# Attention scores as one product over 64 rows instead of two passes over 32, with new turn orders

## The chip, the core and the metric

The kernel runs on one core of a Trainium2 chip. The core's engines work side by side: TensorE (PE in the profile, its weight loads PEld) multiplies, VectorE (DVE) and ScalarE (ACT) work on tiles of 128 partitions, GpSimd (POOL) does elementwise work on SBUF, and SyncE (SP) issues most of the transfers. Products land in PSUM, which has eight banks of 128 x 512 fp32; operands lie in SBUF. The metric is the device time of one execution in microseconds. The run before has three times: 1256.90, 1262.49 and 1262.93, median 1262.49.

## The reference

The input is x of 2 x 1024 x 512 fp32. Three layers follow each other:

```
x = x + 0.5 * ffn(layernorm(x))      # base matmul + bias, and a top-2 mix of 8 rank-16 adapters
x = x + attn(layernorm(x))           # 32 heads of width 16, 8 kv heads, so 4 heads share a k and a v
x = x + 0.5 * ffn(layernorm(x))      # the same ffn again
```

The attention's weights are binarized: each is replaced by its sign, and the row's mean absolute value goes into a scale on the output. Scores are `q.k / sqrt(16)` over all 1024 keys, softmax runs over the keys, and the output projection is binarized too. Outputs that are not finite are replaced.

## The kernel before, in words

**Precision.** fp32 products on TensorE take several passes, the `float32r` format one, with fewer bits. So q and k are split: `y` is the value rounded to float32r (high), `o` the rest (low), and the scores are the sum of the four products of the two halves. For a head of width 16, q's high and low halves lie in 32 rows (16 + 16). A k tile `k` has two planes: plane 0 holds the high half of k, plane 1 the low half, each repeated over all rows. A product of 32 rows of q with the low plane and one with the high plane, both added into the same PSUM bank, give all four terms.

**Staging.** The halves of q and k are written to DRAM by `qkv_part` (`qd`: 2D rows, `kd`: P rows and 2S columns) and read back in the layout of the attention by `place` and, for the first unit alone, `place_k`.

**Units and turns.** The attention is cut into 32 units: a batch (2), a block of 512 queries (2) and a kv head (8) with its four heads. A unit has 32 `m` tiles (128 queries x 512 keys of one head, whose maximum over the keys is taken), 32 `e` tiles (128 keys x 512 queries), and 8 x 2 parts `A` of the product with v. The order within a unit is: `m_tile` on TensorE and `m_max` on VectorE (L751) give a maximum per query; `m_gather` and `m_place` turn it, split into two float32r halves, into two rows per head (`mq`); `e_tile` then computes the transposed scores into a bank, adds the negated maximum by a product of two rows of ones with `mq` (L785), and ScalarE takes the exponential from the bank to SBUF (`es`, L787); `a_part` multiplies with v and a column of ones (L820) into one bank `av`, which `unit_end` copies out (`avs`) and stores.

A unit takes TU = 4 turns of its own, and `e` runs LEAD = 5 turns behind `m`, the `A` parts one turn behind `e`, so each turn holds 8 `m` tiles, 8 `e` tiles and 4 `A` parts of up to three units. Seven PSUM banks rotate among `m`, `e` and the background work; `av` has the eighth.

**Orders written out by hand.** Within a turn, the order of instructions is a string. `m0(5)` is pass 0 of the turn's `m` tile 5, `m1(5)` pass 1; `e0`, `e1` are the two passes of an `e` tile and `e2` its product with `mq`; `A0` to `A3` are the parts with v; `S` is `m_place`. Head h = i % 4 of tile i lies in rows 32h to 32h+31, so tiles of four different heads use four different row strips of TensorE. The other letters offer a place to background work: `F` to one of TensorE, `V`/`W` to VectorE, `C`/`D` to ScalarE.

There are three strings: `FULL` where a background strand wants TensorE, `BARE` where none does, `LEAD_IN` for turns that have `m` only. In the program before, 97 turns are full, 32 bare and 3 lead-in.

**Background.** The rest (the ffn, layernorm, projections, normalization and output projection of other token groups) is written as generators ("strands"). A small planner, `Flow`, decides by costs of its own and by stocks of buffers (`stock`, where `t` counts 512-wide scratch tiles) which strand gets the next place. Planning happens while the program is built; on the chip each engine runs its list in order. All transfers of the attention go through SP's queue, in the order in which the planner issues them: in a turn where a unit ends its `m` tiles, `m_place` first, then other strands' stores, and `place` for the next unit at the turn's end. Of POOL's work the attention needs only `vaug`.

**Buffers.** `q`, `k` and `mq` have three buffers each, `es` fourteen, `av` one bank.

Of the kernel before, what the change touches and what calls it, by code (L numbers as in the profile page):

```python
# [8 lines left out]
F32 = mybir.dt.float32  # L9
F32R = mybir.dt.float32r  # L10
# [5 lines left out]
P = 128  # L16
D = 512
KC = D // P
# [5 lines left out]
REP = H // G  # L24
HD = 16
TG = 4
GT = TG * P
# [5 lines left out]
def macaron_kernel(ctx: ExitStack, tc: tile.TileContext, x_in, wbT, b_base, wrT, aT, bT,  # L33
                   wqT, q_sc, wkT, k_sc, wvT, v_sc, woT, o_sc, out):
    nc = tc.nc
    B, S, _ = x_in.shape
# [4 lines left out]
    const = ctx.enter_context(tc.tile_pool(name="const", bufs=1))  # L41
    xpool = ctx.enter_context(tc.tile_pool(name="xres", bufs=B * NG))
    p2 = ctx.enter_context(tc.tile_pool(name="p2", bufs=2))
    tmp = ctx.enter_context(tc.tile_pool(name="tmp", bufs=11))
    sm = ctx.enter_context(tc.tile_pool(name="sm", bufs=4))
    dram = ctx.enter_context(tc.tile_pool(name="dram", bufs=2, space=bass.MemoryType.DRAM))
    ps = ctx.enter_context(tc.tile_pool(name="ps", bufs=7, space=bass.MemoryType.PSUM))
# [5 lines left out]
    def bank(name):  # L53
        return ps.tile([P, 512], F32, tag="w", name=name)
# [75 lines left out]
    class Flow:  # L130
        def __init__(self):
            self.t, self.free, self.strands, self.n = 0, True, [], 0
            self.stock = dict(m=3, n=4, t=10, xT=2, xL=2, hT=1, fb=6)
            self.lock = None
            self.busy = dict.fromkeys("Pvagd", 0)

# [353 lines left out]
    def qkv_part(b, g, xs, i, fast, at):  # L490
# [40 lines left out]
        if i <= KC:  # L531
            yield "a", "v"
            hi = y[:, :].bitcast(F32R)
            nc.scalar.copy(hi, o)  # L534
            yield "v" if fast else "g", "a"
            lo = o[:, :].bitcast(F32R)
            (nc.vector if fast else nc.gpsimd).tensor_tensor(lo, o, y, ALU.subtract)  # L537
            for j, t in enumerate((y, o)):
                dst = (qd[b][i * 2 * P:(i + 1) * 2 * P, cols].rearrange(
                           "(h i d) s -> h i d s", i=2, d=HD)[:, j, :, :] if i < KC  # L540
                       else kd[b][:, j * S + g * GT:j * S + (g + 1) * GT])
                yield ("d", "v" if fast else "g") if j == 0 else ("d", "d")
                nc.sync.dma_start(dst, t)
        flow.give(t=2 if i <= KC else 1)
        ended.add((b, g, i))

# [72 lines left out]
    def o_proj(b, g, hs, rank, mv, given, fast=False):  # L619
# [32 lines left out]
        for t in range(TG):  # L652
# [7 lines left out]

    FULL = ("e0(3) e0(2) m0(5) m0(0) e1(3) e1(2) m1(5) V m1(0) e2(3) e2(2) C e0(1) A0 A1 A2 A3 S "
            "m0(1) m0(6) e0(7) e0(4) m1(1) m1(6) e1(7) W e1(4) e1(1) m0(2) e2(7) e2(4) e2(1) C "
            "m1(2) V F e0(6) e0(0) m0(7) e0(5) e1(6) e1(0) m1(7) e1(5) e2(6) e2(0) D m0(3) e2(5) "
            "m0(4) m1(3) F m1(4)")
    BARE = ("C m0(1) m0(2) e0(3) e0(4) V m1(1) e0(6) e1(3) e1(4) m0(5) e1(6) e2(4) e2(3) m1(5) "
            "m1(2) A0 S e2(6) e0(1) m0(0) e0(7) e1(1) C m1(0) e1(7) W m0(6) e2(1) e0(0) e2(7) m1(6) "
            "A1 e1(0) V m0(7) e0(5) e0(2) e2(0) D m1(7) e1(2) e1(5) m0(4) m0(3) e2(2) e2(5) m1(4) "
            "m1(3) A2 A3")  # L670
    LEAD_IN = ("m0(0) m0(5) m0(2) V m1(0) m1(5) F C V m0(7) m1(2) m1(7) V F C m0(4) m0(1) m0(6) V m1(4) "
               "m1(1) F C V m0(3) V m1(6) S m1(3) F C V")
    FULL, BARE, LEAD_IN = (
        [(o[0], int(o[1]) if len(o) > 1 else 0, int(o[3]) if len(o) > 2 else 0)
         for o in t.split()] for t in (FULL, BARE, LEAD_IN))
    TU = NT // 2
    LEAD = TU + 1
    units = [(b, qb, g) for b in range(B) for qb in range(NQB) for g in range(G)]
# [3 lines left out]
    def place(u):  # L682


        b, qb, g = units[u]
        q = p2.tile([P, 512], F32R, tag="q", name=f"q{u}", bufs=3)
        nc.sync.dma_start(q.bitcast(F32), qd[b][g * P:(g + 1) * P, qb * 512:(qb + 1) * 512])
        k = p2.tile([P, 2, S], F32R, tag="k", name=f"k{u}", bufs=3)
        st[u].update(q=q, k=k, es={}, mq=p2.tile([P, 512], F32R, tag="mq", name=f"mq{u}", bufs=3),
                     mn=p2.tile([P, REP, 4, 2], F32, tag="mn", name=f"mn{u}"))  # L690
        if u:
            nc.sync.dma_start(k.bitcast(F32).rearrange("p i s -> p (i s)"),
                              kd[b][g * HD:(g + 1) * HD, :].unsqueeze(0).to_broadcast(
                                  [P // HD, HD, 2 * S]))

    def place_k(half):

        for i in range(2):
            nc.sync.dma_start(st[0]["k"].bitcast(F32)[:, i, half * 512:(half + 1) * 512],
                              kd[0][0:HD, i * S + half * 512:i * S + (half + 1) * 512]  # L700
                              .unsqueeze(0).to_broadcast([P // HD, HD, 512]))

    def begin():

        yield "u", lambda: {(0, 0, KC), (0, 0, 0)} <= ended
        yield "d", "x"
        place(0)
        place_k(0)
        for j in range(4):
            yield "P", "d" if j == 0 else "", None, 4  # L710
            for p in range(2):
                for h in range(REP):
                    m_tile(0, j * REP + h, p, False)
            for h in range(REP):
                yield "v", "P"
                m_max(0, j * REP + h)
                flow.give(fb=1)
        yield "u", lambda: (0, 1, KC) in ended
        yield "d", "x"
        place_k(1)  # L720

    def place_v(u):

# [8 lines left out]
        step = i // REP  # L732
        return (step % 4, step // 4) if u == 0 else (step // 2, step % 2)

    def m_tile(u, i, p, end=True):

        s = st[u]
        h, (qt, kh) = i % REP, m_where(u, i)
        rows = slice(32 * h, 32 * h + 32)
        if p == 0:  # L740
            s["m", i] = bank(f"m{u}_{i}")
        nc.tensor.matmul(s["m", i], s["q"][rows, qt * P:(qt + 1) * P],  # L742
                         s["k"][rows, 1 - p, kh * 512:(kh + 1) * 512],
                         start=(p == 0), stop=(p == 1))
        if p == 1 and end:
            m_max(u, i)

    def m_max(u, i):
# [23 lines left out]
    def e_tile(u, i, p):  # L772

        s = st[u]
        kt, h = i // REP, i % REP
        rows = slice(32 * h, 32 * h + 32)
        if p == 0:
            s["e", i] = bank(f"e{u}_{i}")
        t = s["e", i]
        if p < 2:  # L780
            nc.tensor.matmul(t, s["k"][rows, 1 - p, kt * P:(kt + 1) * P], s["q"][rows, :],  # L781
                             start=(p == 0), stop=False)
        else:
            two = slice(32 * h, 32 * h + 2)
            nc.tensor.matmul(t, ones_r[two, :], s["mq"][two, :], start=False, stop=True)  # L785
            e = p2.tile([P, 512], F32, tag="es", name=f"es{u}_{i}", bufs=14)
            nc.scalar.activation(e, s.pop(("e", i)), AF.Exp, scale=HD ** -0.5)  # L787
            s["es"][i] = e
# [42 lines left out]
    def attention(chains, n0):  # L831
# [5 lines left out]
        live = []  # L837

        def need(*keys):
            for _ in range(4000):  # L840
                flow.settle()
                if set(keys) <= ended:
                    return
                flow.t += 1
                for kind in "Pvagd":
                    flow.busy[kind] = 0
                    flow.offer(kind)
            raise RuntimeError([(s.rank, s.kind, s.arg) for s in flow.strands])

        for n in range(n0, TU * len(units) + LEAD + 1):  # L850
# [5 lines left out]
            if e and e[1] == 0:  # L856
                need(*[(units[e[0]][0], h, KC + 1) for h in range(NG)])
                place_v(e[0])
            order = (LEAD_IN if not e and not a else FULL if flow.wants("P", begin + TICK * 5 // 8)
                     else BARE)  # L860

            hold = n % TU == 0 and n // TU
            for pos, (kind, p, i) in enumerate(order):
                flow.t = max(flow.t, begin + pos * TICK // len(order))
                if kind == "m":
                    if m:
                        m_tile(m[0], m[1] * 2 * REP + i, p)
                elif kind == "e":
                    if e:
                        e_tile(e[0], e[1] * 2 * REP + i, p)  # L870
                elif kind == "A":
                    if a:
                        a_part(a[0], a[1] * 2 + p // 2, p % 2)
                elif kind == "S":
                    if 0 < hold <= len(units):
                        m_place(hold - 1)
                    hold = 0
                elif kind == "F":
                    flow.offer("P")
                elif kind in "VW":  # L880
                    if kind == "V" or not m or flow.crowd("v") > 1:
                        flow.offer("v")
                elif kind in "CD":
                    if kind == "C" or not e or flow.crowd("a") > 1:
                        flow.offer("a")
                flow.offer("g")
                if not hold:
                    flow.offer("d")
# [9 lines left out]


    qd = [dram.tile([2 * D, S], F32, tag="qd", name=f"qd{b}") for b in range(B)]  # L900
    kd = [dram.tile([P, 2 * S], F32, tag="kd", name=f"kd{b}") for b in range(B)]
    ad = [dram.tile([G * P, S], F32, tag="ad", name=f"ad{b}") for b in range(B)]
    rv = dram.tile([2, P, 512], F32, tag="rv", name="rv", bufs=1)
    rd = [dram.tile([NQB, H, 512], F32, tag="rd", name=f"rd{b}") for b in range(B)]
# [118 lines left out]
```

## Time and profile before

| what | value |
|---|---|
| times of three runs | 1256.90, 1262.49, 1262.93 us |
| profiled execution | 1256.92 us, span 1255.2 us |
| granted TensorE clock, mean over the span | 0.915 |
| PE busy, DVE busy, ACT busy, POOL busy | 1148.8, 902.8, 641.6, 295.0 us |
| first `e` product to last `av` product | 148.9 to 1185.8 us |
| the same stretch: DVE busy, ACT busy, DMA share, granted clock | 759.1 us, 601.3 us, 0.24, 0.93 |
| DMA moved | 85.57 MB |

The span runs from the first to the last instruction; the time of an execution is about 2 us more. A group line gives the engine, operation, tiles (out<-in), count, then busy time and mean length, then the idle time of the engine before such instructions and what ended it. TensorE's products are pipelined and their ends are modelled, so the distance between starts says more than the length. In the chain of waits, each step is followed back to what released it; "issue" is time in which an engine waited for nothing that the profile shows.

### The profile page before, as it was taken

To read this page: it belongs to the slowest core of one execution; us is meant where nothing else is said; L and a number is where in the kernel's file an instruction comes from. 1 tells how busy PE (TensorE), PEld (TensorE's weight loads), DVE (VectorE), ACT (ScalarE), POOL (GpSimd) and SP (SyncE) were. 2 spreads that over 40 slices of the span, in tenths; PEclk is the share of its full clock that TensorE was granted. 3 is DMA by queue.
4 is the path that set the end of the run, shared out by engine and by line. 5 is a ranking of instruction groups with operands and counts; after the bars stand their busy time and mean duration, and the time that the engine had idled before them with its cause. 6 is when DMAs were issued, how large, how long until landed. Compare 5 with 4: busy or idle time off the path is not lost.

```text
span 1255.2 us, 25499 instructions
## 1 busy us (share of the span) xinstructions
PE 1148.8 (92%) x10501; PEld 606.1 (48%) x10501; DVE 902.8 (72%) x1733; ACT 641.6 (51%) x1249; POOL 295.0 (24%) x302
## 2 busy tenths in 40 slices
PE   3988699999999999999999999999999999998868
PEld 3546355454454544444554445444455444545434
DVE  5578876767786777776677976777769677895273
ACT  2222255655554665565565666455557655566401
POOL 3135832000000340031555220241000300422110
PEclk8989588899986999987999899899989899999788
DMA  7010332121212222223132241122222422211110
GB/s 254 1 59 34 81 122 85 52 52 52 52 52 52 69 80 57 70 76 89 49 90 75 72 122 53 33 52 69 61 60 67 123 68 65 68 55 38 45 39 34
DMA packets 38708, 85.57 MB, mean 68 GB/s; under 512 B 7728, under 2 KB 10800, under 8 KB 34624
## 3 DMA queue, kind: packets, MB, share of 16 engines
q1 hardware_dynamic: 37184, 81.26, 22.4%
q8 instruction: 82, 1.34, 0.4%
q10 hardware_dynamic: 1152, 2.10, 0.4%
q0 software_dynamic: 256, 0.59, 0.3%
q14 instruction: 34, 0.28, 0.1%
HBM read 59.57 MB, written 23.84 MB: 66 GB/s over the span
## 4 chain that ended last, share of the span: by engine, by line
PE 70%; DVE 19%; issue 3%; DMA 2%; POOL 2%; ACT 1%; SPq 1%; POOLq 0%; ACTq 0%; DVEq 0%
PE av L820 20%; PE m L742 16%; DVE mn L751 11%; PE e L781 10%; PE pbf L419 5%; PE pbs L419 5%; PE e L785 4%; PE po L634 2%; PE phs L342 1%; DMA qd<-y 1%; PE pq L504 1%; PE pbf L423 1%; PE pv L521 1%; PE pbs L423 1%; DMA x<-in_x 1%
## 5 line engine op out<-in xcount | busy, mean ns | idle before, releaser
L751 DVE TENSOR_REDUCE mn<-m 128x1 f32<-128x512 f32 x1024 | 657.0, 682 | 230.0 <-PE m L742 221.4
L787 ACT ACTIVATE es<-e 128x512 f32<-128x512 f32 x1024 | 546.9, 599 | 425.6 <-PE e L785 401.4
L742 PE MATMUL m<-k,q 32*128 32x512 f32 x2048 | 492.1, 464 | 21.1 <-DVE mn L751 15.1
L781 PE MATMUL e<-q,k 32*128 32x512 f32 x2048 | 407.9, 474 | 8.3 <-DVE mn L751 6.9
L742 PEld LDWEIGHTS m<-k,q 32*128 32x128 f32 x2048 | 240.8, 196 | 153.0 <-issue 67.4
L820 PE MATMUL av<-es,vaug 128*32 128x256 f32 x4096 | 290.3, 416 | 16.4 <-issue 10.3
L781 PEld LDWEIGHTS e<-q,k 32*128 32x128 f32 x2048 | 185.1, 194 | 114.7 <-DVE mn L751 69.6
L785 PE MATMUL e<-mq,ones_r 2*128 2x512 f32 x1024 | 233.0, 431 | 3.7 <-DMA mq<-mT 3.7
L820 PEld LDWEIGHTS av<-es,vaug 128*32 128x32 f32 x4096 | 121.5, 116 | 154.5 <-issue 103.8
L785 PEld LDWEIGHTS e<-mq,ones_r 2*128 2x128 f32 x1024 | 125.6, 196 | 25.1 <-issue 13.7
L419 PE MATMUL pbf<-wb,xTf 128*128 128x512 f32 x128 | 68.9, 653 | 1.3 <-DVE mn L751 1.3
L419 PE MATMUL pbs<-wb,xTs 128*128 128x512 f32 x128 | 64.8, 618 | 1.2 <-DVE mn L751 1.2
L586 POOL TENSOR_TENSOR an<-an,rb 128x512 f32<-128x512 f32 x15 | 19.2, 1281 | 142.7 <-DMA rd<-rs 72.1
L249 POOL TENSOR_SCALAR loa<-y 128x512 f32<-128x512 f32 x17 | 12.7, 750 | 157.1 <-ACT y L509 147.5
L726 POOL MEMSET vaug<- 128x128 f32 x32 | 6.6, 206 | 137.7 <-PE av L820 137.6
L419 PEld LDWEIGHTS pbf<-wb,xTf 128*128 128x128 f32 x128 | 23.2, 203 | 30.1 <-issue 26.1
L419 PEld LDWEIGHTS pbs<-wb,xTs 128*128 128x128 f32 x128 | 21.5, 189 | 27.1 <-issue 22.9
L253 POOL TENSOR_SCALAR z<-y 128x512 f32<-128x512 f32 x17 | 34.1, 2008 | 1.8 <-DMA qd<-y 0.6
L249 POOL TENSOR_SCALAR loo<-yo 128x512 f32<-128x512 f32 x12 | 7.4, 613 | 113.7 <-DVE yo L639 110.0
L537 POOL TENSOR_TENSOR z<-z,y 128x512 fp32r<-128x512 f32 x17 | 21.9, 1293 | 51.0 <-ACT y L534 51.0
L590 POOL TENSOR_TENSOR anxL<-an,anxT 128x512 fp32r<-128x512 f32 x15 | 19.2, 1280 | 53.5 <-ACT anxT L588 53.4
L634 PE MATMUL po<-sign_o,anxT 128*128 128x512 f32 x64 | 29.4, 459 | 1.2 <-DVE mn L751 1.2
(193 smaller groups left out, 1008.3 us busy)
## 6 DMA issues: line engine op xcount, KB each, us to landing
k<-kd SPq DMA_DIRECT2D x31, 1024.0 KB
q<-qd SPq DMA_DIRECT2D x32, 256.0 KB
ad<-avs SPq DMA_DIRECT2D x32, 256.0 KB
x<-in_x SPq DMA_DIRECT2D x16, 256.0 KB
qd<-y SPq DMA_DIRECT2D x16, 256.0 KB
qd<-z SPq DMA_DIRECT2D x16, 256.0 KB
an<-ad SPq DMA_DIRECT2D x15, 256.0 KB
rb<-rd SPq DMA_DIRECT2D x15, 256.0 KB
```

The source lines that it names most:

```text
L249: nc.gpsimd.tensor_scalar(lo_, y, 0.0, -BIG, ALU.min, ALU.max)
L253: nc.gpsimd.tensor_scalar(o, y, 0.0, BIG, ALU.max, ALU.min)
L419: nc.tensor.matmul(pb, xT[:, c, t * P:(t + 1) * P], wb[:, c, :], start=(c == 0), stop=False)
L423: nc.tensor.matmul(pb, hT[0][:, t * P:(t + 1) * P], lb, start=False, stop=True)
L537: (nc.vector if fast else nc.gpsimd).tensor_tensor(lo, o, y, ALU.subtract)
L634: nc.tensor.matmul(po, hs[j][:, c, t * P:(t + 1) * P], wo[:, c, :], start=(c + j == 0), stop=(c + j == KC))
L742: nc.tensor.matmul(s["m", i], s["q"][rows, qt * P:(qt + 1) * P], s["k"][rows, 1 - p, kh * 512:(kh + 1) * 512], start=(p == 0), stop=(p == 1))
L751: nc.vector.tensor_reduce(s["mn"][:, h, qt, kh:kh + 1], s.pop(("m", i)), AX.X, ALU.max, negate=True)
L781: nc.tensor.matmul(t, s["k"][rows, 1 - p, kt * P:(kt + 1) * P], s["q"][rows, :], start=(p == 0), stop=False)
L785: nc.tensor.matmul(t, ones_r[two, :], s["mq"][two, :], start=False, stop=True)
L787: nc.scalar.activation(e, s.pop(("e", i)), AF.Exp, scale=HD ** -0.5)
L820: nc.tensor.matmul(s["av"][32 * h:32 * h + 32, cols], s["v"][:, kt, :], s["es"][kt * REP + h][:, cols], start=(kt + half == 0), stop=(kt + ...
```

## The change

- q's halves lie twice in 64 rows: the tile `q` has a plane for each parity of the head, and heads 0 and 1 use rows 0 to 63, heads 2 and 3 rows 64 to 127. For a head the rows are high, low, high, low of q.
- k lies in 64 rows as high, high, low, low, twice over the partitions, in one plane. One product over 64 rows gives the four terms; the second pass is gone for `m` and for `e`.
- The product with `mq` keeps its two rows in the 32-row strip of the head. It is now `e1`.
- q and k share one buffer of the size that k had. q is loaded by four transfers, each of which reads 32 rows twice; k by one of half the size. `kd` now has 4P rows of S columns, and each half is stored twice, by two transfers.
- The scratch pool has 13 tiles instead of 11, and the planner's stock `t` is 12 instead of 10.
- All three strings are new. In them, `F` stands twice side by side in `FULL`, and `A0` of `BARE` stands near the start of the turn, so the planner first waits until the bank `av` of the unit before has been copied. In the program after, 95 turns are full, 34 bare and 3 lead-in. `FULL` is chosen by the place of its first `F`.

```diff
-    tmp = ctx.enter_context(tc.tile_pool(name="tmp", bufs=11))
+    tmp = ctx.enter_context(tc.tile_pool(name="tmp", bufs=13))
...
-            self.stock = dict(m=3, n=4, t=10, xT=2, xL=2, hT=1, fb=6)
+            self.stock = dict(m=3, n=4, t=12, xT=2, xL=2, hT=1, fb=6)
...
-                dst = (qd[b][i * 2 * P:(i + 1) * 2 * P, cols].rearrange(
-                           "(h i d) s -> h i d s", i=2, d=HD)[:, j, :, :] if i < KC
-                       else kd[b][:, j * S + g * GT:j * S + (g + 1) * GT])
-                yield ("d", "v" if fast else "g") if j == 0 else ("d", "d")
-                nc.sync.dma_start(dst, t)
+                n_ = 2 if i < KC else 4
+                dst = (qd[b][i * 2 * P:(i + 1) * 2 * P, cols] if i < KC else kd[b][:, cols]).rearrange(
+                    "(h i d) s -> h i d s", i=n_, d=HD)
+                for c in range(n_ // 2):
+                    yield ("d", "v" if fast else "g") if j + c == 0 else ("d", "d")
+                    nc.sync.dma_start(dst[:, j * n_ // 2 + c, :, :], t)
...
-    FULL = ("e0(3) e0(2) m0(5) m0(0) e1(3) e1(2) m1(5) V m1(0) e2(3) e2(2) C e0(1) A0 A1 A2 A3 S "
-            "m0(1) m0(6) e0(7) e0(4) m1(1) m1(6) e1(7) W e1(4) e1(1) m0(2) e2(7) e2(4) e2(1) C "
-            "m1(2) V F e0(6) e0(0) m0(7) e0(5) e1(6) e1(0) m1(7) e1(5) e2(6) e2(0) D m0(3) e2(5) "
-            "m0(4) m1(3) F m1(4)")
-    BARE = ("C m0(1) m0(2) e0(3) e0(4) V m1(1) e0(6) e1(3) e1(4) m0(5) e1(6) e2(4) e2(3) m1(5) "
-            "m1(2) A0 S e2(6) e0(1) m0(0) e0(7) e1(1) C m1(0) e1(7) W m0(6) e2(1) e0(0) e2(7) m1(6) "
-            "A1 e1(0) V m0(7) e0(5) e0(2) e2(0) D m1(7) e1(2) e1(5) m0(4) m0(3) e2(2) e2(5) m1(4) "
-            "m1(3) A2 A3")
+    FULL = ("m0(5) V m0(3) C F F e0(4) m0(7) V W e0(1) e0(3) e1(1) e1(4) e0(2) e1(2) e1(3) m0(1) C "
+            "A0 A1 S e0(6) e0(0) e1(6) e0(5) m0(6) e1(0) e1(5) m0(2) D A2 A3 m0(4) e0(7) m0(0) "
+            "e1(7)")
+    BARE = ("e0(0) W m0(2) A0 S C e0(3) e1(0) e0(2) m0(4) e1(2) e1(3) m0(1) A1 A2 m0(0) C m0(7) "
+            "e0(1) e0(6) e0(4) e1(6) e1(4) D e1(1) m0(6) A3 m0(5) V e0(7) e0(5) m0(3) e1(5) e1(7) V")
+    LEAD_IN = ("m0(0) m0(5) m0(2) V m0(7) F C V m0(4) m0(1) V F C m0(6) V F C V m0(3) V S F C V")
...
-        q = p2.tile([P, 512], F32R, tag="q", name=f"q{u}", bufs=3)
-        nc.sync.dma_start(q.bitcast(F32), qd[b][g * P:(g + 1) * P, qb * 512:(qb + 1) * 512])
-        k = p2.tile([P, 2, S], F32R, tag="k", name=f"k{u}", bufs=3)
+        qk = p2.tile([P, 2, S], F32R, tag="k", name=f"k{u}", bufs=3)
+        q, k = qk[:, 0, :].rearrange("p (t s) -> p t s", t=2), qk[:, 1, :]
...
+        for t in range(2):
+            for h in range(2):
+                row = g * P + (2 * h + t) * 32
+                nc.sync.dma_start(q.bitcast(F32)[64 * h:64 * h + 64, t, :],
+                                  qd[b][row:row + 32, qb * 512:(qb + 1) * 512].unsqueeze(0)
+                                  .to_broadcast([2, 32, 512]))
...
+    def place_k(u, s0, s1):
+        b, _, g = units[u]
+        nc.sync.dma_start(st[u]["k"].bitcast(F32)[:, s0:s1],
+                          kd[b][g * 64:(g + 1) * 64, s0:s1].unsqueeze(0).to_broadcast(
+                              [2, 64, s1 - s0]))
...
+    def rows_of(h):
+        return slice(64 * (h // 2), 64 * (h // 2) + 64)
+
+    def m_tile(u, i, end=True):
...
-        nc.tensor.matmul(s["m", i], s["q"][rows, qt * P:(qt + 1) * P],
-                         s["k"][rows, 1 - p, kh * 512:(kh + 1) * 512],
-                         start=(p == 0), stop=(p == 1))
+        nc.tensor.matmul(s["m", i], s["q"][rows_of(h), h % 2, qt * P:(qt + 1) * P],
+                         s["k"][rows_of(h), kh * 512:(kh + 1) * 512], start=True, stop=True)
...
-        if p < 2:
-            nc.tensor.matmul(t, s["k"][rows, 1 - p, kt * P:(kt + 1) * P], s["q"][rows, :],
-                             start=(p == 0), stop=False)
+            nc.tensor.matmul(t, s["k"][rows_of(h), kt * P:(kt + 1) * P], s["q"][rows_of(h), h % 2, :],
+                             start=True, stop=False)
...
                     if a:
+                        if a[0] and a[1] == p == 0:
+                            until(lambda: "av" not in st[a[0] - 1])
                         a_part(a[0], a[1] * 2 + p // 2, p % 2)
...
-    kd = [dram.tile([P, 2 * S], F32, tag="kd", name=f"kd{b}") for b in range(B)]
+    kd = [dram.tile([4 * P, S], F32, tag="kd", name=f"kd{b}") for b in range(B)]
```

## The prediction

> **What bounds the kernel now.** The page's busy lines and its chain come first.
>
> ```profile
> PE 1148.8 (92%) x10501; PEld 606.1 (48%) x10501; DVE 902.8 (72%) x1733; ACT 641.6 (51%) x1249; POOL 295.0 (24%) x302
> ...
> PE 70%; DVE 19%; issue 3%; DMA 2%; POOL 2%; ACT 1%; SPq 1%; POOLq 0%; ACTq 0%; DVEq 0%
> PE av L820 20%; PE m L742 16%; DVE mn L751 11%; PE e L781 10%; PE pbf L419 5%; PE pbs L419 5%; PE e L785 4%; PE po L634 2%; PE phs L342 1%; DMA qd<-y 1%; PE pq L504 1%; PE pbf L423 1%; PE pv L521 1%; PE pbs L423 1%; DMA x<-in_x 1%
> ```
>
> TensorE carries 70% of the chain, the row maximum `mn` (L751) on VectorE 11%, or 0.109 x 1255.2 = 137 us by the finer share of the chain view. The first product of `e` starts at 148.9 us and the last `av` ends at 1185.8 us: 1037 us for 132 turns, 7.86 us each. Next, the chain in order of time inside one full turn (start, us, what):
>
> ```profile
> 293.27 1.87 PE av L820 x32
> 295.14 0.43 PE m L742 x2
> 295.57 0.01 PE e L781
> 295.57 0.23 PE m L742
> 295.80 0.00 PE e L781
> 295.80 0.00 PE m L742
> 295.81 0.22 PE e L781
> 296.03 0.24 PE e L785 x3
> 296.26 0.00 PE m L742
> 296.27 1.06 PE pbf L419 x2
> 297.32 0.42 PE e L781 x2
> ```
>
> Score products come in sets of up to four, one per 32 rows, that start together; sets follow each other at 0.23 us. The first step after `av` or `pbf` costs 0.43 us. So a **change of tile shape** (32x128 score tiles, 128x32 `av`, 128x128 background) costs 0.43 - 0.23 = 0.20 us. The timeline of TensorE shows it product by product (start, length, group):
>
> ```profile
> 602.75 0.50 PE L504 MATMUL pq<-xTa,sign_k 128*128 128x512 f32 x1
> 603.09 0.40 PE L504 MATMUL pq<-xLa,sign_k 128*128 128x512 f32 x1
> 603.32 0.39 PE L504 MATMUL pq<-xTa,sign_k 128*128 128x512 f32 x1
> 603.55 0.40 PE L504 MATMUL pq<-xLa,sign_k 128*128 128x512 f32 x1
> 603.88 0.49 PE L781 MATMUL e<-q,k 32*128 32x512 f32 x2
> 603.88 0.49 PE L742 MATMUL m<-k,q 32*128 32x512 f32 x1
> ```
>
> Inside one shape the starts are 0.23 apart; from `pq` (128 rows) to `e` (32 rows) 0.33, and the step behind a change is 0.34 (602.75 to 603.09): 0.10 + 0.11 = 0.21 us. No change of shape in this trace is free. Two-row `mq` products (L785) beside 32-row ones at 604.45 cost nothing: both fill one 32-row strip. The group lines give what is exchanged:
>
> ```profile
> L742 PE MATMUL m<-k,q 32*128 32x512 f32 x2048 | 492.1, 464 | 21.1 <-DVE mn L751 15.1
> L781 PE MATMUL e<-q,k 32*128 32x512 f32 x2048 | 407.9, 474 | 8.3 <-DVE mn L751 6.9
> L785 PE MATMUL e<-mq,ones_r 2*128 2x512 f32 x1024 | 233.0, 431 | 3.7 <-DMA mq<-mT 3.7
> ```
>
> **The change part by part.**
>
> *Fewer, taller products.* 2048 + 2048 products of a quarter set become 1024 + 1024 of half a set; the 1024 `mq` products keep their quarter. Before: 5120/4 = 1280 full sets; after: 2048/2 + 1024/4 = 1280. Counting through the two built orders, with a new set whenever rows collide or another kind of work comes between, gives 1399 and 1396: 3 x 0.23 = -1 us. 2048 weight loads of 0.19 us go too; they lie beside running products (0.23 us between sets with four loads inside it), so they give 0; were that cover gone, a load would show as the 0.10 us after a change of shape.
>
> *Shape changes already known.* In the two orders the changes among score, `av`, background and `mp` go from 776 to 795 (two background offers now stand side by side, `av` is cut into more pieces): 19 x 0.20 = +4 us.
>
> *Shape changes that are new.* `m` and the first `e` product are now 64 rows high, the `mq` product still lies in 32. The built order goes between the two heights 1199 times (5 groups of `mq` in a full turn, 4 in a bare one, two changes each; 95 full and 34 bare turns). The trace has no such pair. Lower bound 0, from the two-row products above that join 32-row ones for nothing; upper bound 0.20 us each, as every change of shape that it has, plus the sets torn: a 32-row pair can't share a set with a 64-row product then, and the count is 1865 sets for 1396. I take the upper end, since the nearest rows are changes of tile height (128 to 32) and these cost 0.20 without exception: 1199 x 0.20 = 240, 469 x 0.23 = 108, together +348 us.
>
> The Trainium skill, page "TensorEngine Tiling (Array Packing)", section "Tiling Modes", says that a change of tiling mode, not of tile alone, drains TensorE, and lists 64 and 32 rows as different modes. The page "TensorE: Matmul & The Clock Gate", Part 3, says that weight loads pass running products where the row groups differ; by that one alone mixed heights on disjoint rows would cost nothing and the sum would end near the value before.
>
> *Banks.* A score bank of `m` is held for one step less, 0.23 of about 1.5 us (two steps, 0.39 of a product, 0.68 of the reduction), 15%. TensorE's weight loads waited 49.4 + 69.6 us on `mn` and 12.2 + 10.9 us on `es`, 142 us in all: 0 to -142, and 15% of it, -20 us, is what I take where TensorE's own work stays equal. Where it grows by 348/132 = 2.6 us a turn, VectorE's 759/132 = 5.75 us per turn are hidden in 10.5 and most of the 137 us of `mn` on the chain go: bounds 0 and -137, I take two thirds, -91, and nothing for the banks beside it.
>
> *av early in a bare turn.* A0 of a unit now stands near the start of a bare turn and must wait for the copy of the bank before it (`avs`, 0.60 us, behind up to three `es` of 0.60). About 8 of the 32 units start so: 0 to 8 x 2.4 = 19, I take +5 us. Behind the wait stand all later products.
>
> *Loads and stores.* Per unit q comes as four 128 KB loads instead of one of 256 KB, k as 512 KB for 1024; k stores double. Bytes: -31 x 0.5 + 32 x 0.25 + 1 = about -6.5 MB of 85, with the DMA engines at 0.24 in the attention. SP issues three more loads, 0.33 us each (one `q` issue is 0.33, one `k` 0.62): 1 us later for k and for what queues behind, against three turns (23 us) until `m` of the next unit reads it. 0; without that cover 32 us. Two more `kd` stores before the attention, 0.61 us each on SP: +1. No DMA of POOL's queue moves.
>
> *Two more scratch tiles, other lead-in.* The planner may start background steps a little earlier (`t` 12 for 10). The first three units of the attention took 37, 36 and 35 us against 30.6 of an all-full one in the middle, while background on VectorE and POOL ran beside them: 0 to -17 us. I take 0, since the same work is still done there. The lead-in's three turns hold half the `m` products at twice the height: 0.
>
> **The sum.** The profiled execution took 1256.9 us (span 1255.2). 1256.9 - 1 + 4 + 348 - 91 + 5 + 1 = 1523 us. The median of the three runs lies 5.6 us above the profiled one, so I forecast 1528 us; a difference under 0.5% (6 us, the spread of the three runs) can't be told from no change.
>
> **The rivals** (against the median).
>
> *Mixed heights are free.* For it: rows that don't overlap start within 0.01 us of each other in every set, and strips hold two or 32 rows at will. Against: every change of height seen costs. TensorE's work is then what it was: 1262.5 - 1 + 4 - 20 + 5 + 1 = 1252, and up to 30 us less if the new order also removes a fifth of the 142 us of waits: about 1240. This is the case on the other side. It decides from the point where a change of height costs under 0.02 us (25/1199).
>
> *Only the rows that overlap wait.* A change then stalls one half of the array while the other streams on. Going through the built order, each product as soon as its own rows are free and 0.20 us where they last held another height, the attention needs 145 us more; with a third of the 137 us of `mn` gone, 1262.5 + 145 - 45 = 1362.
>
> *The clock falls too.* With gaps at each change TensorE may be granted less: 0.93 over the attention now, 0.78 between 150 and 180 us. At 0.82 TensorE's work without the changes of shape (1865 sets of 0.23, `av` and background, 823 us in all) takes 823 x (0.93/0.82 - 1) = 110 us more: 1640. It is the upper part of the forecast's own range, for which 1430 (a change at half price, -120) to 1640 stands.
>
> **How the numbers follow.** Full stall at every change of height 0.42 (forecast, 1528); overlap only 0.14 (1362); free 0.44, of which 0.27 faster by over 0.5%, 0.07 within it, and 0.10 slower, where the order with its later banks and the early A0 costs more than the shorter hold gives. Slower 0.42 + 0.14 + 0.10 = 0.66. The range must reach into the free case: from 1230 (which leaves 0.1 below it) to 1625 (0.08 above).
>
> **What would show it.** In the timeline of after, `e` on 64 rows followed by `mq`: a start 0.33 and not 0.23 behind the last, and weight loads idle for 0.36 us on "issue" before them; a full turn near 10 us instead of 7.35; `mn` nearly gone from the chain, VectorE busy under 62%. If instead a 64-row product and two `mq` products start within 0.01 us of each other, heights mix freely and the forecast is wrong by the whole 348 us. If `mq` products start 0.33 us behind their own half while the other half goes on at 0.23, it is the middle rival. q and k loads on the chain would break the step on loads.

## The result, and the profile after

The changed kernel takes 1681 us (median of four runs, 1655 to 1698) against 1262 us. Two of the four, 1692 and 1698 us, fell into a slower state with a lower granted clock, so comparisons go by the other two, 1655 and 1670 us, mean 1663: a ratio of 1.319, 95% interval 1.307 to 1.331. The direction is as forecast, the size is not: 1663 as well as 1681 lies above the range's end of 1625.

The profiled execution of after has a span of 1653.4 us, 398 more than before. It splits by the first `e` and the last `av` product, and by the clock records of the trace, which hold only two values, full and half:

| | before | after | difference | in the prediction |
|---|---|---|---|---|
| ahead of the first `e` product, us | 148.9 | 177.5 | +28.6 | +1 |
| attention, us | 1036.9 | 1399.6 | +362.7 | +265 |
| behind the last `av` product, us | 69.4 | 76.3 | +6.9 | 0 |
| TensorE at half clock in the attention, us | 152.5 | 484.7 | +332 | in a rival only |

The page of after, its busy line and its chain:

```profile
PE 1556.1 (94%) x8453; PEld 708.2 (43%) x8453; DVE 937.3 (57%) x1733; ACT 654.2 (40%) x1249; POOL 291.8 (18%) x302
...
PE 86%; DVE 5%; DMA 3%; issue 2%; POOL 2%; ACT 1%; SPq 1%; POOLq 0%; DVEq 0%; ACTq 0%
PE av L817 19%; PE e L782 18%; PE e L777 17%; PE m L742 17%; PE pbs L419 3%; PE pbf L419 3%; DMA k<-kd 2%; PE po L635 2%; PE pq L504 1%; DVE mn L750 1%; PE phs L342 1%; PE pbs L423 1%; DMA x<-in_x 1%; PE pbf L423 1%; PE pv L521 1%
```

TensorE carries 86% instead of 70%, the row maximum 1% instead of 11% (0.8% of 1653.4, or 13 us for 137): VectorE's waits went under, as the prediction had it. The product with `mq` (L782) went from 4% to 18% with the same count. Its weight loads now wait on "issue" (busy, mean, then idle before and its cause):

```profile
L782 PE MATMUL e<-mq,ones_r 2*128 2x512 f32 x1024 | 342.8, 567 | 0.3 <-DMA mq<-mT 0.3
...
L782 PEld LDWEIGHTS e<-mq,ones_r 2*128 2x128 f32 x1024 | 125.3, 206 | 209.3 <-issue 209.3
```

The chain of after in order of time (start, length, what), first at half clock (granted clock 0.50 from 300 to 307.6 us), then at full clock (1.00 from 322 to 328 us):

```profile
304.73 0.72 PE e L782 x2
305.45 0.72 PE e L777
306.18 0.72 PE e L782 x2
306.90 0.72 PE m L742
...
323.51 0.43 PE e L777 x2
323.94 0.43 PE e L782
324.37 0.43 PE e L777
324.80 0.44 PE e L782 x2
325.24 0.43 PE m L742
```

At full clock each set stands alone between two changes of height and takes 0.43 us, not 0.23: the forecast's 0.20 us per change to the hundredth. Units of four full turns take 40.0 us at full clock, 10.0 a turn ("near 10 us" in the prediction; 30.6 a unit before). What the sum left out stands in the upper lines: at half clock the same step takes 0.72 us.

### The profile page after: what moved, and what is told of

It reads as the page before. It is cut to its first block, busy times and chain, and to the rows that moved or that the text cites. A ratio compares the mean times of both kernels' runs of the same rounds, so it can differ in the third digit from the quotient of the medians.

```text
span 1653.4 us, 21725 instructions
## 1 busy us (share of the span) xinstructions
PE 1556.1 (94%) x8453; PEld 708.2 (43%) x8453; DVE 937.3 (57%) x1733; ACT 654.2 (40%) x1249; POOL 291.8 (18%) x302
## 4 chain that ended last, share of the span: by engine, by line
PE 86%; DVE 5%; DMA 3%; issue 2%; POOL 2%; ACT 1%; SPq 1%; POOLq 0%; DVEq 0%; ACTq 0%
PE av L817 19%; PE e L782 18%; PE e L777 17%; PE m L742 17%; PE pbs L419 3%; PE pbf L419 3%; DMA k<-kd 2%; PE po L635 2%; PE pq L504 1%; DVE mn L750 1%; PE phs L342 1%; PE pbs L423 1%; DMA x<-in_x 1%; PE pbf L423 1%; PE pv L521 1%
## 5 line engine op out<-in xcount | busy, mean ns | idle before, releaser
L750 DVE TENSOR_REDUCE mn<-m 128x1 f32<-128x512 f32 x1024 | 682.6, 687 | 590.8 <-PE m L742 461.2
L784 ACT ACTIVATE es<-e 128x512 f32<-128x512 f32 x1024 | 557.3, 598 | 784.9 <-PE e L782 784.9
L742 PE MATMUL m<-k 64*128 64x512 f32 x1024 | 473.0, 564 | 35.1 <-DMA k<-kd 31.7
L777 PE MATMUL e<-k 64*128 64x512 f32 x1024 | 408.5, 531 | 1.2 <-ACT es L784 0.7
L817 PE MATMUL av<-es,vaug 128*32 128x256 f32 x4096 | 336.7, 447 | 9.4 <-issue 8.3
L782 PE MATMUL e<-mq,ones_r 2*128 2x512 f32 x1024 | 342.8, 567 | 0.3 <-DMA mq<-mT 0.3
L742 PEld LDWEIGHTS m<-k 64*128 64x128 f32 x1024 | 179.1, 214 | 224.8 <-issue 135.7
L777 PEld LDWEIGHTS e<-k 64*128 64x128 f32 x1024 | 162.7, 214 | 181.7 <-issue 93.9
L782 PEld LDWEIGHTS e<-mq,ones_r 2*128 2x128 f32 x1024 | 125.3, 206 | 209.3 <-issue 209.3
L817 PEld LDWEIGHTS av<-es,vaug 128*32 128x32 f32 x4096 | 114.1, 120 | 146.9 <-issue 115.8
L646 POOL TENSOR_TENSOR x<-x,ro 128x512 f32<-128x512 f32 x12 | 15.3, 1273 | 145.2 <-DVE ro L259 133.4
```

The costliest lines, as they stand in the source:

```text
L742: nc.tensor.matmul(s["m", i], s["q"][rows_of(h), h % 2, qt * P:(qt + 1) * P], s["k"][rows_of(h), kh * 512:(kh + 1) * 512], start=True, sto ...
L750: nc.vector.tensor_reduce(s["mn"][:, h, qt, kh:kh + 1], s.pop(("m", i)), AX.X, ALU.max, negate=True)
L777: nc.tensor.matmul(t, s["k"][rows_of(h), kt * P:(kt + 1) * P], s["q"][rows_of(h), h % 2, :], start=True, stop=False)
L817: nc.tensor.matmul(s["av"][32 * h:32 * h + 32, cols], s["v"][:, kt, :], s["es"][kt * REP + h][:, cols], start=(kt + half == 0), stop=(kt + ...
```

## The experiments

The theory after this result: (1) every change between 64 and 32 rows stalls the whole array by 0.20 us at full clock; (2) the array then has too few rows at work, the clock is halved, and this has a price of its own; (3) the loads that read their rows twice are slow. Rivals: the 64-row products or the new orders are slow in themselves; only overlapping rows wait; the clock falls for idle time, not for rows.

**Products alone** (`m1`). Stretches of float32r products of 512 columns on 64-row halves `H`, 32-row strips `Q` and two rows `T`, none waiting for another engine:

```
dense32:  Q0 Q1 Q2 Q3      dense64:  H0 H1           disjoint: H0 Q2 Q3
overlap:  H0 Q0 Q1         turns:    H0 H1 T0 T1     one64: H0     one32: Q0     two: T0 T1 T2 T3
```

> A kernel of TensorE products alone (none of the reference's work; its output is not the reference's): stretches of 100 to 150 repetitions on float32r operands of 512 columns, with 80 products over all 128 rows between them to bring the clock back. If every change of tile height stalls the whole array: four 32-row products 0.22 us a set, two 64-row products 0.22 us a set, and 0.86 us for each repetition of a 64-row product and two 32-row ones, the same whether the 32-row ones lie in the other half (disjoint) or in the same one (overlap), 1.44 us once the clock has halved. If only overlapping rows wait: 0.22 us for the disjoint repetition and 0.86 for the overlapping one. For the clock: if it follows how many rows work, a single 64-row or 32-row stream without any change of height ends at half clock (0.43 us a product); if it follows only whether products run at all, both stay at 0.22.

Busy time by windows, one for each stretch (window, its length, busy time and count by engine, granted clock): the first 4.4 us of `disjoint`, all of it, `overlap`, `one32`, `one64`, `two`, `dense32`, `dense64`; then 124 us of `turns`.

```profile
135.10:139.50 4.40, 4.40 (x17) 1.95 (x16) 0.00 (x0) 0.00 (x0) 1.00 0.00 0
135.10:275.80 140.70, 140.70 (x301) 55.72 (x300) 0.00 (x0) 0.00 (x0) 0.52 0.00 0
296.40:437.60 141.20, 141.20 (x299) 55.84 (x298) 0.00 (x0) 0.00 (x0) 0.51 0.00 0
673.20:731.80 58.60, 58.60 (x151) 44.96 (x150) 0.00 (x0) 0.00 (x0) 0.55 0.00 1
620.60:654.60 34.00, 34.00 (x151) 27.53 (x150) 0.00 (x0) 0.00 (x0) 1.00 0.00 0
753.00:812.60 59.60, 59.60 (x598) 50.87 (x600) 0.00 (x0) 0.00 (x0) 0.54 0.01 1
29.90:63.80 33.90, 33.90 (x601) 33.65 (x600) 0.00 (x0) 0.00 (x0) 1.00 0.01 2
82.50:116.40 33.90, 33.90 (x301) 27.98 (x300) 0.00 (x0) 0.00 (x0) 1.00 0.00 1
475.00:599.00 124.00, 124.00 (x344) 49.05 (x342) 0.00 (x0) 0.00 (x0) 0.50 0.00 0
```

Sets of one height follow at 33.9/150 = 0.23 us, for 32 rows as for 64. A repetition of a 64-row product and two 32-row ones takes 140.7/100 = 1.41 us whether the 32-row ones lie in the other half or the same one: the rival "only overlapping rows wait" is out. `turns`, the pattern of after, takes 124/86 = 1.44 us at half clock, 0.72 a step. In its first 4.4 us, still at full clock, `disjoint` starts a new step every 0.43 us; the weight loads of its disjoint rows don't run ahead either, each starts with its own product. This is one execution of each stretch.

For the clock, two things count. One stream of 64 rows keeps the full clock; one stream of 32 rows, which never pauses either, falls to half within 6 us, and so do sets of two-row products: so rows at work count. Stalls count too: each step of `disjoint` has 64 rows at work, as `one64` has, but starts only every 0.43 us, and its clock is halved after 5 us.

The Trainium skill, page "TensorE: Matmul & The Clock Gate", Part 1, explains the halved clock by how busy TensorE has been lately, and lets idle windows bring it about. The two single streams were busy all the time and got 1.00 and 0.55: the measurement adds the rows at work. The page "TensorEngine Tiling (Array Packing)", section "Tiling Modes", states the drain at a change of mode; `disjoint` agrees, 64 against 32 rows included.

**One height for all** (`e1`). After, with the `mq` product over 64 rows: ones in its two rows and zeros in the others, against a tile that is zero elsewhere.

```diff
...
-            two = slice(32 * h, 32 * h + 2)
-            nc.tensor.matmul(t, ones_r[two, :], s["mq"][two, :], start=False, stop=True)
+            nc.tensor.matmul(t, sel[rows_of(h), h % 2, :], s["mq"][rows_of(h), :], start=False, stop=True)
```

> The changed kernel with the mq product over 64 rows (ones in its two rows and zeros in the others against a tile that is zero elsewhere), so no change between 64 and 32 rows is left; all else, orders and loads too, stays. If the changes of height are the cause: TensorE's own work in the attention falls from 1222 to 934 us (1199 changes and the torn sets go, 2 sets a turn come), the granted clock goes back to about 0.9, and the time is 1270 to 1330 us. If the 64-row products, the new orders or the new loads are the cause: over 1550 us, clock near 0.83.

Measured: 1291 us, ratio 1.020 (1.011 to 1.029), clock 0.93; the attention takes 1039.8 us, 360 less than in after. One edit that makes two rows into 64 takes 372 us off (1663 to 1291). It removes the changes of height and the two-row products at once; `e8` below parts them. 64-row products, the orders and the loads together keep 1 to 3%.

**Fewer changes of height** (`e2`). After, with the eight `mq` products of a turn in two groups of four. `FULL` as an example:

```diff
-"m0(5) m0(3) F F e0(4) m0(7) e0(1) e0(3) e1(1) e1(4) e0(2) e1(2) e1(3) m0(1) A0 A1 S e0(6) ..."
+"m0(5) m0(3) F F e0(4) m0(7) e0(1) e0(3) m0(1) e0(2) e1(1) e1(4) e1(2) e1(3) A0 A1 S e0(6) ..."
```

> The changed kernel with other orders: in each turn the eight mq products stand in two groups of four, so the two heights change 290 times instead of 1199, counted in the built order (all changes of shape 1084 for 1994), and the sets are fuller. If changes of height are the cause, TensorE's own work falls from 1222 to 901 us, and the time is 1250 to 1320 us with the clock near 0.9. If it is the 64-row products or the loads: over 1550 us.

Measured: 1452 us, ratio 1.150 (1.141 to 1.159). The direction is right, the size is missed by over 130 us: the attention took 1203.5 us, 314 of them at half clock. The grouped order is taken up again below (`e10`).

**Plain loads** (`e3`). The changed kernel's loads read 32 or 64 rows twice (`to_broadcast([2, ...])`), so their outermost dimension is two. Cut into two loads each:

```diff
...
-        nc.sync.dma_start(st[u]["k"].bitcast(F32)[:, s0:s1],
-                          kd[b][g * 64:(g + 1) * 64, s0:s1].unsqueeze(0).to_broadcast([2, 64, s1 - s0]))
+        for c in range(2):
+            nc.sync.dma_start(st[u]["k"].bitcast(F32)[64 * c:64 * c + 64, s0:s1],
+                              kd[b][g * 64:(g + 1) * 64, s0:s1])
```

> The changed kernel with each load that reads its rows twice cut into two plain loads (8 for q and 2 for k per unit). After showed k loads moved at 51 GB/s with the DMA engines at 0.13, and two waits of 16.6 and 20.8 us for k ahead of the attention. If the doubled reading is what makes them slow, these waits fall to 5 to 10 us each and the first e product comes 15 to 25 us earlier than in the changed kernel (177.5 us): about 1660 us. If it is something else, the first e product stays at 177 us or comes later by the additional issues (5 of 0.55 us per unit).

Measured: 1637 us, ratio 1.293 (1.280 to 1.306), the first `e` product at 154.6 us, 22.9 earlier. The windows over the loads (last columns: granted clock, share of the 16 DMA engines, GB/s), first of after while q and k loads run, then of this kernel during its own:

```profile
90.00:102.00 12.00, 4.49 (x18) 2.35 (x16) 5.63 (x12) 2.12 (x4) 2.38 (x5) 0.86 0.13 52
```

```profile
86.00:92.00 6.00, 6.00 (x16) 2.65 (x15) 3.20 (x8) 0.00 (x0) 0.70 (x1) 1.00 0.46 129
```

0.13 is two of sixteen DMA engines (0.13 x 16 = 2.1): loads whose outermost dimension is two kept two engines' worth busy, at 52 GB/s. In the chain of after this showed as two pieces, both ahead of the attention and both gone here:

```profile
88.35 16.59 DMA k<-kd
...
148.29 20.77 DMA k<-kd
```

The Trainium skill, page "DMA: Bandwidth & Descriptors", section "Rules for kernel authors", says so: an outermost dimension below 16, as of a leading broadcast, confines a transfer to at most that many engines. The two windows agree with it.

**Both repairs** (`e4`). One height and plain loads:

> The changed kernel with both single repairs together: the mq product over 64 rows, and each doubled load cut into two plain ones. If the changes of height and the doubled loads are the whole loss, the first e product comes near 155 us, the attention takes 1035 to 1045 us as with equal heights alone, and the time is 1255 to 1280 us, within 1.5% of the kernel before. If something else of the change costs (new orders, taller products, more issues on SP), it stays above 1285 us.

Measured: 1181 us, ratio 0.937 (0.930 to 0.943), 78 us faster than the kernel before. The expectation missed by over 70 us, to the good side. With equal heights TensorE is fast enough for the slow loads to be seen in the attention as well. They head the chain of `e1`, and its waits have a line (total, times, longest) of which 33.9 us lie in the attention; with plain loads 0.3 us are left.

```profile
DMA k<-kd 17%; PE av L823 14%; PE m L749 10%; PE e L784 9%; PE e L788 7%; PE pbs L426 3%; DVE mn L757 3%; PE pbf L426 3%; DMA rd<-rs 3%; DMA rb<-rd 2%; SPq L698 2%; PE po L642 1%; PE pq L511 1%; DMA x<-in_x 1%; PE pv L528 1%
```

```profile
PE m L749 <- DMA k<-kd: 63.5, 14, 15.3
```

The attention fell from 1039.8 to 948.9 us, its half-clock time from 95.6 to 3.4 us. The two kernels differ in their loads alone, with the same rows at work, so waiting costs clock too. The change carried a gain that its two faults hid, although TensorE has two sets a turn more (132 x 2 x 0.23 = 61 us) than before. Not all of the 78 us is the change's own: the kernel before gains as well when its `mq` product is padded with zeros (1232 us, `e7` below), and against that kernel 1181 us is 4% less.

**Without the product with `mq`** (`e5`). q high, low, high (48 rows) and the two rows of the negated maximum beside k high, high, low and ones: one product of 50 rows gives `e`. The product of the two low halves is left out.

```diff
...
-            nc.tensor.matmul(t, s["k"][rows_of(h), kt * P:(kt + 1) * P], s["q"][rows_of(h), h % 2, :],
-                             start=True, stop=False)
+            nc.tensor.matmul(t, s["k"][rows_of(h, 50), kt * P:(kt + 1) * P],
+                             s["q"][rows_of(h, 50), h % 2, :], start=True, stop=True)
```

> A version without the mq product: a head's 64 rows hold q high, low, high (48 rows) and the two rows of the negated maximum; those of k hold high, high, low and ones. m multiplies 48 rows, e 50 rows, both in 64-row tiles; the product of the two low halves is left out. Loads are plain, without doubled reading; orders as in the changed kernel with the mq places empty. TensorE's own work in the attention falls from 874 us before to 815. If TensorE still sets the pace, 59 us come off and the time is 1180 to 1220 us. If VectorE takes over (759 us of work in an attention of 1037 us, so 1 - 759/1037 of slack), less: 1220 to 1260.

Measured: 1153 us, ratio 0.915 (0.910 to 0.920): better than expected by 27 us, as its base was. The next run (`e6`) lays the score products out in eight sets a turn.

> As e5_one_product, with full and bare orders laid out so that the 16 score products of a turn fill eight sets instead of nine: TensorE's own work 786 us for 815. If TensorE sets the pace, another 20 to 29 us come off against e5_one_product; if VectorE does, under 10 us.

Measured: 1149 us, ratio 0.911 (0.905 to 0.916). The intervals of the two overlap, so the 29 us of counted work can't be seen; under 10 us was the sign named for VectorE setting the pace. Half-clock time in the attention went up, from 72.6 to 100.4 us. How the two share the loss wasn't measured.

**Rows of zeros.** Three kernels test the clock: the products and their order stay, only rows of zeros join in. In the kernel before, the `mq` product over its whole strip (`e7`):

```diff
...
-            two = slice(32 * h, 32 * h + 2)
-            nc.tensor.matmul(t, ones_r[two, :], s["mq"][two, :], start=False, stop=True)
+            strip = slice(32 * h, 32 * h + 32)
+            nc.tensor.matmul(t, ones_r[strip, :], s["mq"][strip, :], start=False, stop=True)
```

> The kernel before with one edit: the product with mq goes over the whole 32-row strip of its head (ones against a tile that is zero outside the two rows), so 30 rows of zeros work beside the two. The number of products, their order and the waits stay. If the granted clock follows how many rows work, as the single 64-row stream (full clock) and the two-row sets (half clock) of the kernel of products alone say, TensorE's half-clock time in the attention falls from 152 us to under 80 and the time falls by 15 to 50 us, to 1210 to 1245. If rows of zeros don't count, or the clock falls for idle time alone, there is no change: 1250 to 1270.

The same in after with plain loads (`e8`):

> The changed kernel with plain loads (e3_loads_cut, 1637 us) and the mq product over its whole 32-row strip. All 1199 changes of height stay. If rows at work set the clock, half-clock time in the attention falls from 503 us and with it the time by 40 to 150 us, to 1490 to 1600; a unit of four full turns at full clock stays at 40 us. If the price of the changes doesn't depend on the clock, or zero rows don't count, 1620 to 1655.

And 64 rows instead of 48 and 50 in the version without `mq` products, by rows of zeros in q, which are stored and loaded with it (`e9`):

> e6_one_product_orders (1149 us) with rows of zeros up to 64 in each score product instead of 48 (m) and 50 (e). If rows at work set the clock, half-clock time in the attention falls from 100 us to under 40, and the time by 10 to 40 us, to 1110 to 1140. If not, 1140 to 1155.

| kernel | without zeros, us | with, us | half clock in the attention, us | attention, us |
|---|---|---|---|---|
| before | 1263 | 1232 (ratio 0.975, 0.971 to 0.979) | 152.5 to 79.8 | 1036.9 to 1014.7 |
| after, plain loads | 1637 | 1562 (ratio to before 1.230, 1.224 to 1.236) | 503.5 to 314.0 | 1408.2 to 1331.0 |
| one product | 1149 | 1125 (ratio to before 0.890, 0.887 to 0.893) | 100.4 to 29.4 | 916.1 to 889.7 |

All three lie where rows at work set the clock, none where zeros don't count. In the first pair nothing but the zeros differs (`mq` lies in three fixed tiles, cleared once), and it is 2.5% faster. In the second all changes of height stay and a unit of four full turns at full clock still takes 40.0 us; the 314.0 us left at half clock show that the zeros cure only a part. The windows over the two attentions, before and then with the strips (granted clock third from the end):

```profile
148.90:1185.80 1036.90, 985.65 (x9875) 508.46 (x9874) 759.12 (x1402) 601.07 (x1155) 219.42 (x226) 0.93 0.24 67
```

```profile
146.40:1161.10 1014.70, 959.57 (x9875) 498.51 (x9874) 758.68 (x1402) 600.82 (x1155) 219.37 (x226) 0.96 0.24 68
```

A microsecond at half clock cost 77.2/189.5 = 0.41 us in the second pair, 0.31 and 0.37 in the others; all three are estimates, by two profiled executions each. The last kernel is the best one seen: 11% below the kernel before.

**The grouped order again** (`e10`), with plain loads and strips:

> e2_grouped (1452 us; 290 changes of height, half-clock time 314 us in the attention) with the two repairs that showed an effect: plain loads, and the mq product over its 32-row strip. Its TensorE work was counted as 901 us against an attention of 1203. If the miss of e2 (1452 for 1250 to 1320) was the half clock and the doubled loads, half-clock time falls below 150 us and the time to 1300 to 1370. If it was that four mq products in a row make the banks and VectorE wait, it stays above 1400 us.

Measured: 1378 us, ratio 1.095 (1.090 to 1.099). Half-clock time fell to 131 us, so clock and loads were some 74 us of the miss; the time is still 8 us over the range that was to tell. Units of four full turns take 34 us at full clock, as in `e2`, for 30.6 in the kernel before, though the counted TensorE work is only 27 us more over all 32 units (901 for 874). The row maximum is back at 11% of the chain (1% in after), and in the order of time a group of `mq` products leaves sets half empty or waits for it:

```profile
489.53 0.43 PE e L779
...
490.03 0.70 DVE mn L752
...
490.77 0.49 PE e L779
491.27 0.43 PE e L784 x2
```

That this comes of seven banks held longer by a group of four is argued, not shown.

**The scratch tiles** (`e11`). `e4` with 11 tiles and `t` 10:

> e4_equal_loads (1181 us) with the scratch pool and the planner's stock of the kernel before (11 tiles, t 10). If the two more scratch tiles carry a part of the 78 us by which e4 beats the kernel before, the time rises to 1195 or more; if not, 1175 to 1190.

Measured: 1192 us, ratio 0.946 (0.943 to 0.949) against 0.937 (0.930 to 0.943) for `e4`: between the two expectations, some 10 of the 78 us.

## Why the prediction was right or wrong

- *What bounds the kernel.* Right: TensorE's path set the time, and a longer TensorE path took VectorE's waits with it.
- *New shape changes, +348 us.* Mechanism and price were right: 0.43 us a step, 10.0 us a full turn, the whole array stalled (`disjoint` equals `overlap`). The upper end, taken from the nearest rows, was the true one.
- *The clock.* This is the step that failed. The sum took the granted clock as it was and put its fall into a rival, at 0.82 and 110 us; it came out at 0.83 in the attention. The 332 us more at half clock cost an estimated 101 to 136 us, by the 0.31 to 0.41 us of the three pairs; the steps give (0.72 - 0.43)/0.72 = 0.40. The rival's reason, gaps at each change, is one part (`disjoint` against `one64`); the other, few rows at work in the `mq` products, the prediction didn't name (`e8`: half-clock time from 503.5 to 314.0 us). The profile of before held the price: at half clock from 690.5 to 697.3 us, its first step behind `av` takes 0.73 us and the next ones 0.42.

```profile
691.87 0.73 PE e L781 x2
692.60 0.42 PE e L785
693.02 0.42 PE m L742
```

- *VectorE's waits, -91 us.* Too small: the row maximum's share of the chain fell from 137 to 13 us, so 124 us went, close to the bound of 137. The attention grew by 363 us where the sum has 265; with 33 us more of waits gone, 131 us are left for the clock, within the estimate above.
- *Loads and stores, +1 us.* Wrong. Bytes and issues were counted, not the engines that serve them. Two pieces of 16.6 and 20.8 us on the chain end in k loads, with q's slow loads ahead of them; the first `e` product came 28.6 us late, and plain loads took 22.9 us of it back. The cover of 23 us held in after, because TensorE was slow; with one height it did not.
- *Two more scratch tiles, 0.* By one profiled execution of `e11` and of `e4`, they delay the first `e` product (155.0 us for 148.5) and shorten the attention (948.9 us for 962.1).
- *Banks, -20 us, and the free rival at 1240 us.* Too small. Without changes of height and with proper loads the rest of the change gives 1181 us, and the row maximum keeps 84 us of the chain (7.1% of 1180) for 137, though TensorE has 61 us more of sets. A large part of the 78 us is clock: 149 us less at half clock (152.5 to 3.4) are an estimated 46 to 61 us. Some 10 us go with the scratch tiles; how the remainder splits between the one-step products and the new orders wasn't measured.
- *av early, +5 us; the tail.* Not tested. The part behind the last `av` product is 4 to 7 us longer in every variant of after; why stays open.
- *The chances.* Slower at 0.66 was the right side; the range ended 38 us below 1663. The clock rival alone, at 1640, lay beyond it, and clock and loads, the two unknowns that could only add, were not added to each other. The 1430 given for half price doesn't come out of the sum either: 1528 - 120 = 1408.

## What to carry to other kernels

Mixing tile heights on TensorE costs a full stall of the array at each change, also where the rows are disjoint; make all products of a mixed stream one height, by zeros if need be. Read the granted clock beside the step length in each stage: a stream that keeps few rows at work, or stalls often, may lose half its clock, and padding with zero rows can win a part of it back. For a transfer that reads rows several times, look at its outermost dimension and at the DMA share while it runs, not at its bytes.

## What had not been expected of the hardware

- Rows of zeros speed a kernel up: 1263 to 1232 us in the kernel before, with the same products in the same order.
- A stream of 32-row products without a pause is granted half the clock (0.55 over 58.6 us), one of 64 rows the full one (1.00 over 34 us); for a stream without a pause the border lies between.
- A change of height costs 0.20 us at full clock and 0.72 - 0.43 = 0.29 us at half, so the stall is longer at the slower clock but does not double.
